# A finer rank for every step of a stage, and eight products of zeros at the start, in a Toeplitz mixer with FFN

## The chip, the cores and the metric

The kernel runs on one core of a Trainium2 chip. The time is the device time of one execution in microseconds (us). Each core has five engines that run side by side, each with its own queue that is worked off strictly in order: TensorE (PE, products into PSUM), VectorE (DVE), ScalarE (ACT), GpSimd (POOL) and SyncE (SP, which here only issues loads and stores). Weight loads of PE are shown as PEld; they overlap the products.

## The reference

The input is x with 4 batches of 2048 tokens of 256 numbers, in float32. One layer is computed:

```python
x = x + attn(_layernorm(x))
x = x + ffn(_layernorm(x))

# attn, a gated Toeplitz mixer
uv = jax.nn.silu(x @ uv_w)                 # (.., 512)
u, v = jnp.split(uv, 2, axis=-1)
out = (u * _tno(v, rpe_params)) @ o_w

# _tno: a convolution over the 2048 tokens of each channel, both directions
a = concatenate([t_zero, t_pos, 0, t_neg]) # 4096 taps per channel
y = irfft(rfft(a) * rfft(v, n=4096))[:2048]

# taps: a small network of the position, times a decay
h = pos @ rpe_pos_w
for i in range(3):
    h = silu(ln(h, w[i], b[i])) @ rpe_fc_w[i]
taps = silu(ln(h, ..)) @ rpe_out_w * 0.99 ** |pos|

# ffn: 8 groups of 1024 tokens, each with its own two matrices and no nonlinearity
h1 = einsum('gmh,goh->gmo', xg, W1) + b1
h2 = einsum('gmo,gho->gmh', h1, W2) + b2
```

## The kernel before, in words

**Tiling.** Tokens lie on the 128 partitions. A batch is cut into four quarters of 512 tokens (q = 0 to 3), the 256 channels into two halves (h = 0, 1). The long convolution is cut, by additions on DVE, into 8 "rings" (r = 0 to 7), each a transform of length 256 done as products with a constant matrix.

**Stages.** All are Python functions that only record operations:

- `rpe_network` (line 540): the position network for all 4096 positions, four layers one after the other. A layer is two products `ph`, their squares and copies on ACT, sixteen small products `pvar` that sum the squares, an inverse root on DVE (`inverse_root`, line 524, three Newton steps of small operations), its spread `ne` (DVE), eight transposes `pr` (PE), two products on DVE and the activation `z` (ACT), which feeds the next `ph`.
- `rpe_transform` (line 617): the taps' transform by rings: products `hp`, a DVE product `tr`, products `pa`, and copies into the constant tables `amd` and `am0` to `am6`.
- `stage_a` (line 495), for each batch and quarter: load x (`xa`), mean and variance (`statistics`, line 367; on DVE for batch 0, on ACT for the others), the power -1/2 on POOL (`rs`), normalisation on ACT (`xn`), eight transposes (`pt_a`), copies (`xnt`), the products `pv` with the value half of uv_w, silu, and sums on POOL (`c`).
- `prepare` (line 759), for each batch and half: 16 pieces of DVE additions that make the eight rings.
- `gate` (line 781): the products `pu` and silu, the gate `gt`.
- `stage_b` (line 791): for each ring a `forward` (products `pf` and, on DVE, the complex product with the table: two products `y` and `far`, then two sums into `y`), a `backward` (products `acc`) and an `after` on DVE; `end` combines the rings on DVE into four tiles `tk`, which POOL multiplies into the gates.
- `stage_w` (line 722), for each of the 8 FFN groups: the two matrices are multiplied with each other, `pw`, in four chunks (o = 0, 2, 4, 6) of 256 KB of W1 and 256 KB of W2 each. A chunk has `WB = 2` buffers; its W1 half is shifted by a bias on ACT before the four products. The result is `wt`.
- `stage_d` (line 927), for each batch and quarter: load x again, products `po` with o_w, add, layernorm as in stage a, transposes `pt_d`, products `pff` with `wt`, add, store.

**What sets the order.** The order of the instructions is made by a planner, `issue_order` (line 220). It knows which operation reads what another writes, the buffers of each pool, and an estimated duration of each (`Operation.cost`, line 116). It then plays the program through: of all operations whose inputs and buffers are there, the one that can start earliest goes next, and among those that can start at the same time the one of the lowest rank. A rank is a number from the table `PLACE`, plus 20 for each batch:

```python
at, _, _, k = min((at, ops[k].engine == "POOL", rank[k], k) for w in waiting.values() for k in w if (at := earliest(k)) is not None)
```

The ranks also set the order in which the tiles of a pool get their buffers. In the kernel before, all operations of one call of a stage share one rank: loading, statistics, transposes and products of a quarter of stage a, the load of the matrix, the products and the DVE steps of a ring. Only `prepare`, `end`, `stage_w` and `stage_d` are cut into pieces (at each `yield`) that have ranks of their own.

The resulting order is what the chip runs. All instructions are issued at line 1019, so the profile shows that line for nearly all of them, and tiles tell them apart.

Of the kernel before, what the change touches and what calls it, by code (L numbers as in the profile page):

```python
# [106 lines left out]
class Operation:  # L107
# [8 lines left out]
    def cost(self, method):  # L116

        n, psum = columns(self.outs[0]), [a.space == PSUM for a in self.ins]
        if self.dma:
            return (400 if self.engine == "SP" else 460), n * P * 4 / 250  # L120
# [20 lines left out]
class Pool:  # L141
# [5 lines left out]
    def tile(self, shape, dtype, name, **kw):  # L147
# [5 lines left out]

PLACE = {
    "a first": (-99.0, -98.0, -97.0, -96.0),
    "a": (1.74, -2.67, 2.51, 4.46),
    "b": (
        (6.26, 12.16, 4.1, 8.11, 8.37, 13.79, 12.58, 14.11),
        (10.46, 20.27, 15.97, 19.01, 18.94, 18.98, 20.74, 20.97),
    ),  # L160
    "d": (
        (25.35, 27.7),
        (26.25, 28.74),
        (30.44, 33.54),
        (29.38, 31.46),
    ),
    "d last": (
        (42.27, 25.3),
        (65.21, 140.66),
        (46.22, 27.3),  # L170
        (61.26, 28.3),
    ),
    "e": (
        (14.31, 18.21, 18.05, 16.77, 63.85, 71.2, 77.59, 18.72, 12.6, 21.84, 13.2),
        (20.2, 20.5, 20.8, 19.37, 21.4, 39.89, 22.0, 22.54, 22.6, 28.52, 26.75),
    ),
    "e last": (20.2, 100.83, 20.8, 21.1, 21.4, 111.26, 22.0, 22.3, 22.6, 22.9, 23.2),
    "f": (
        (2.08, 2.91, 1.13, 2.05, 4.0, 3.57, 6.5, 6.26),
        (4.04, 18.16, 13.91, 14.02, 14.8, 14.19, 17.79, 18.04),  # L180
    ),
    "g first": (
        (-95.0, 1.77, -95.0, -40.12),
        (-95.0, -95.0, -95.0, -95.0),
    ),
    "g": (
        (6.27, 12.71, 15.72, 5.68),
        (13.81, 10.75, 16.06, 24.4),
    ),
    "p first": (21.76, -4.4, -4.1, -3.8, -3.5, -23.28, -84.19, -2.6, -2.3, -2.0, -1.7, -1.4, -1.1, -0.8, -0.5, 5.66),  # L190
    "p": (
        (55.79, 1.74, 22.08, 23.91, 1.63, 19.64, 38.78, 19.76, 4.06, 16.19, 4.2, 33.43, 39.59, 10.38, 4.51, 33.61),
        (14.03, 5.6, 11.32, 67.54, 11.67, 6.8, 14.31, 16.92, 15.07, 18.9, 70.61, 20.64, 18.53, 20.4, 45.22, 86.73),
    ),
    "rpe": -100.0,
    "rpet": -10.0,
    "w": (-52.41, -95.4, 43.06, 31.0, 55.36, 77.26, 90.91, 188.4),
# [3 lines left out]
def place(stage, *i):  # L201
    if stage in ("rpe", "rpet"):
        return (PLACE[stage],)
    if stage == "w":
        return (PLACE["w"][i[0]] + 0.1 * i[1],) if i[0] < WT else (PLACE["w"][i[0]] + i[1],)
    b, *i = i
    if b == 0 and (stage in ("a", "g") or (stage == "p" and i[0] == 0)):
        stage, i = stage + " first", i[1:] if stage == "p" else i
    elif b == B - 1 and (stage == "d" or (stage == "e" and i[0] == 1)):
        stage, i = stage + " last", i[1:] if stage == "e" else i  # L210
    at = PLACE[stage]
    for n in i:
        at = at[min(n, len(at) - 1)]
    return (20 * b + at,)


# [3 lines left out]
def issue_order(ops, tags):  # L220
# [43 lines left out]
    while len(order) < len(ops):  # L264
# [5 lines left out]
        free[o.engine] = at + o.busy  # L270
        end = at + o.busy + o.tail
# [24 lines left out]
def kernel(  # L296
# [49 lines left out]
    am_c = [const.tile([P, 2, 2, 2, P], F32, name=f"am{r}") for r in range(NR)]  # L346

# [147 lines left out]
    def stage_a(b, q):  # L495
        xnt = xnts[b, q] = tok.tile([P, 2, 4 * P], F32, tag="xnt", bufs=4, name=f"xnt_{b}_{q}")
        xt = early.pop((b, q), None) or load_x(b, q, "xa")
        name = f"a{b}_{q}"
        transposed(normalized(xt, *statistics(xt, name, on_scalar=b > 0), name), xnt, name)
# [11 lines left out]
        r, j0 = divmod(2 * q, 4)  # L511
        for h in range(2):
            lo, hi = (v[:, :, i, h * P : (h + 1) * P] for i in range(2))
            c = cts[b, h]
            G.tensor_tensor(c[:, r, j0 : j0 + 2, 0, :], hi, lo, ALU.add)
            a_, b_ = (lo, hi) if r else (hi, lo)
            G.tensor_tensor(c[:, 1 - r, j0 : j0 + 2, 1, :], a_, b_, ALU.subtract)
# [22 lines left out]
    def rpe_network():  # L540
# [7 lines left out]
        early.update({(0, q): load_x(0, q, "xa") for q in range(2)})  # L548
        decay = t4("decay", "f4")[:, :NT]
        S.dma_start(decay, decays)  # L550

# [17 lines left out]
        for i in range(L + 1):  # L569
            sqs, ds = [], []  # L570
# [25 lines left out]

        z = t4("z", "i4").rearrange("p (j f) -> p j f", f=F)
# [10 lines left out]
    def load_phases():  # L608
        phs = [io.tile([P, 4, D], F32, tag="xd", name=f"ph_{i}") for i in range(2)]
# [7 lines left out]
    def rpe_transform(z, phs):  # L617
# [62 lines left out]
        for r in range(NR + 1):  # L680
            m = ring_mats(r, 0, f"rpe_{r}")
            ph = ps_f.tile([P, 2 * P], F32, tag="pf", name=f"hp{r}")
# [15 lines left out]
            for k in range(2):  # L698
# [12 lines left out]
                elif k:  # L711
                    A.copy(am_c[r - 1][:, :, :, k, :], src)
                else:
                    V.tensor_copy(am_c[r - 1][:, :, :, k, :], src)

# [6 lines left out]
    def stage_w(g):  # L722
        na, oc = INTER // P, 2
        yield
# [4 lines left out]
        S.dma_start(row, b2[g : g + 1, :].partition_broadcast(P))  # L729
        d = small.tile([P, na], F32, tag="d", bufs=2, name=f"dw_{g}")  # L730
# [4 lines left out]
        for o in range(0, na, oc):  # L735
            w1s = io.tile([P, oc, D], F32, tag="w1", bufs=WB, name=f"w1_{g}_{o}")
            S.dma_start(w1s, w1[g].rearrange("(p a) h -> p a h", a=na)[:, o : o + oc, :])
            w2s = io.tile([P, oc, D], F32, tag="w2", bufs=WB, name=f"w2_{g}_{o}")
            S.dma_start(w2s, w2t[g].rearrange("(p a) h -> p a h", a=na)[:, o : o + oc, :])
# [382 lines left out]
```

## Time and profile before

| | us |
|---|---|
| three runs | 589.31, 589.51, 590.65 (median 589.51) |
| the profiled execution | 589.18 |
| its span, first to last instruction | 587.3 |
| PE busy in the span | 563.2 (96%), 2620 records |
| DVE busy | 504.4 (86%), 1118 records |
| ACT busy | 312.8 (53%) |
| POOL busy | 149.7 (25%) |
| moved by DMA | 81.36 MB, mean 139 GB/s |

The profiled execution is one more execution, 0.3 us under the median of the three runs. A product in float32 appears as two records of PE, a transpose as one. Records overlap, so a record's own duration is longer than the time until the next one starts; where a stretch is dense, the distance of the starts is the cost. Records of one kind that follow each other are merged into one line with their number (x16).

### The profile page before, as it was taken

How to read it: one execution, taken by the hardware profiler on the slowest of the kernel's cores; microseconds unless marked ns; L12 is line 12 of the kernel's file. 1: busy time of each engine (PE TensorE's matmuls, PEld its weight loads, DVE VectorE, ACT ScalarE, POOL GpSimd, SP SyncE). 2: the span in 40 equal slices, each digit the busy share in tenths (PEclk: the TensorE clock that was granted, in tenths of full speed). 3: DMA queues.
4: the chain of work that ended last, by engine and by line, in shares of the span. 5: the costliest groups of instructions: out<-in, count | busy, mean ns of one | idle time of the engine just before them, and what ended most of it. 6: DMA issues, size and time to landing. Idle time of an engine off the chain costs nothing.

```text
span 587.3 us, 8243 instructions
## 1 busy us (share of the span) xinstructions
PE 563.2 (96%) x2620; PEld 457.3 (78%) x2620; DVE 504.4 (86%) x1118; ACT 312.8 (53%) x822; POOL 149.7 (25%) x184
## 2 busy tenths in 40 slices
PE   6899999999997999999999999999999999998797
PEld 3788565887885888787878888778888888787686
DVE  3575984999998799999986999998979999999862
ACT  2779862164322754996545728886348365112162
POOL 0154210011362211123475200106271100020420
PEclk9999999999999999999999999999999999999999
DMA  8731374555454445363541453455443543424202
GB/s 266 204 113 61 89 230 154 157 165 161 142 146 136 109 145 171 108 228 114 157 119 46 153 179 127 145 179 145 125 108 90 193 158 143 149 67 138 78 37 108
DMA packets 39987, 81.36 MB, mean 139 GB/s; under 512 B 5636, under 2 KB 7172, under 8 KB 39944
## 3 DMA queue, kind: packets, MB, share of 16 engines
q1 hardware_dynamic: 39208, 79.91, 44.2%
q10 hardware_dynamic: 736, 0.92, 0.5%
q8 instruction: 21, 0.34, 0.2%
q14 instruction: 22, 0.18, 0.1%
HBM read 72.43 MB, written 8.39 MB: 138 GB/s over the span
## 4 chain that ended last, share of the span: by engine, by line
PE 88%; DMA 7%; ACT 2%; DVE 1%; issue 1%; SPq 0%; ACTq 0%; DVEq 0%
PE acc L1019 18%; PE pf L1019 18%; PE pff L1019 9%; PE pv L1019 9%; PE po L1019 9%; PE pw L1019 7%; PE pu L1019 7%; DMA w<-in_L_ffn_W_dram 6%; PE pt_a L1019 2%; PE pa L1019 2%; PE pt_d L1019 2%; PE ph L1019 2%; PE pvar L1019 1%; PE hp L1019 1%; PE pr L1019 1%; DMA lag_t<-in_lag_rows_dram 1%
## 5 line engine op out<-in xcount | busy, mean ns | idle before, releaser
L1019 PE MATMUL acc<-mats,y 128*128 128x256 f32 (+1 forms) x512 | 114.7, 367 | 0.0
L1019 PEld LDWEIGHTS acc<-mats,y 128*128 128x128 f32 x512 | 91.7, 190 | 14.0 <-issue 2.1
L1019 PE MATMUL pw<-w,w 128*128 128x256 f32 x256 | 65.9, 388 | 11.5 <-DMA w<-in_L_ffn_W_dram 9.7
L1019 POOL TENSOR_TENSOR gt<-gt,tk 128x512 f32<-128x512 f32 x32 | 44.8, 1411 | 122.8 <-DVE tk L1019 122.8
L1019 POOL TENSOR_TENSOR c<-v 128x256 f32<-128x256 f32 x64 | 55.5, 894 | 56.2 <-ACT v L1019 45.8
L1019 PEld LDWEIGHTS pw<-w,w 128*128 128x128 f32 x256 | 46.8, 194 | 21.9 <-ACT w L1019 13.6
L1019 PE MATMUL pv<-uvw,xnt 128*128 128x256 f32 x256 | 60.7, 382 | 0.0
L1019 PE MATMUL po<-ow,gt 128*128 128x256 f32 x256 | 60.2, 379 | 0.0
L1019 ACT ACTIVATE w<-w,dw 128x256 f32<-128x256 f32 x64 | 29.6, 502 | 56.9 <-DMA w<-in_L_ffn_W_dram 56.9
L1019 PE MATMUL pu<-xnt,uvw 128*128 128x512 f32 x128 | 59.8, 592 | 0.0
L1019 PE MATMUL pf<-ra,mats 128*128 128x256 f32 x256 | 58.9, 380 | 0.0
L1019 PE MATMUL pff<-wt,xn 128*128 128x256 f32 x256 | 58.0, 380 | 0.3 <-ACT xn L1019 0.3
L1019 PEld LDWEIGHTS pv<-uvw,xnt 128*128 128x128 f32 x256 | 47.4, 190 | 8.3 <-ACT xnt L1019 1.2
L1019 PEld LDWEIGHTS pf<-ra,mats 128*128 128x128 f32 x256 | 48.2, 190 | 7.0 <-issue 0.5
L1019 PEld LDWEIGHTS pff<-wt,xn 128*128 128x128 f32 x256 | 48.1, 190 | 6.8 <-ACT xn L1019 0.6
L1019 PEld LDWEIGHTS po<-ow,gt 128*128 128x128 f32 x256 | 47.8, 190 | 7.0 <-issue 1.0
L1019 DVE TENSOR_TENSOR y<-y,far 128x256 f32<-128x256 f32 x128 | 51.8, 445 | 0.2
L1019 POOL TENSOR_TENSOR rs_a<-ve_a,mhalf 128x4 f32<-128x4 f32 x16 | 19.8, 1236 | 113.3 <-ACT ve_a L1019 105.2
L1019 POOL TENSOR_TENSOR rs_d<-ve_d,mhalf 128x4 f32<-128x4 f32 x16 | 16.6, 1037 | 115.4 <-ACT ve_d L1019 99.2
L1019 DVE TENSOR_TENSOR y<-pf,am 128x512 f32<-128x512 f32 x56 | 38.3, 684 | 6.5 <-PE pf L1019 5.0
L1019 ACT COPY e<-acc 128x512 f32<-128x512 f32 x24 | 14.0, 584 | 50.5 <-PE acc L1019 43.6
L1019 DVE TENSOR_TENSOR far<-pf,am 128x512 f32<-128x512 f32 x56 | 38.1, 681 | 0.2
(151 smaller groups left out, 1022.0 us busy)
## 6 DMA issues: line engine op xcount, KB each, us to landing
mats<-in_mats_dram SPq DMA_DIRECT2D x128, 256.0 KB, 2.7
w<-in_L_ffn_W_dram SPq DMA_DIRECT2D x64, 256.0 KB, 4.2
xa<-in_x_dram SPq DMA_DIRECT2D x18, 512.0 KB, 3.7
xd<-in_x_dram SPq DMA_DIRECT2D x14, 512.0 KB, 3.5
out_dram<-xd SPq DMA_DIRECT2D x12, 512.0 KB, 2.7
mats_rpe<-in_mats_dram SPq DMA_DIRECT2D x8, 256.0 KB, 4.1
row<-in_L_ffn_b_dram SPq DMA_DIRECT2D x8, 128.0 KB, 4.8
ph<-in_phases_dram SPq DMA_DIRECT2D x4, 256.0 KB, 5.5
```

The costliest lines, as they stand in the source:

```text
L1019: ops[k].call(*ops[k].args, **ops[k].kw)
```

## The change

Four things are edited.

1. Eight products of a tile of zeros (128x256) into a PSUM tile that nothing reads are put at the head, with rank -199. The PSUM tile shares the one buffer of `pw`. A memset of 128x256 on DVE makes the zeros.
2. `PLACE` becomes a flat table with dotted keys. `place` looks up the longest key that is in the table, with " first" for batch 0 and " last" for batch 3, and falls back to shorter keys ("b.1.4.p" to "b.1.4" to "b.1" to "b").
3. Each stage is cut finer: stage a into load (x), statistics and normalisation (n), transposes (t), products (v) and sums (c); a ring into the matrix load (m), the products (p) and the DVE steps (y), forward (f) and backward (b); stage w into loads (l), bias (d), products (m) and the final sum (s), for each chunk; stage d into load, output products (o), statistics (n), transposes (t), FFN products (f) and store (s); each network layer and each ring of the table's transform has a rank of its own.
4. The planner's estimates: a DMA takes its real number of partitions at 270 instead of 128 at 250, and a product that starts in the first 7500 ns counts double.

No operation of the computation is removed or added; buffers and their numbers stay.

```diff
-            return (400 if self.engine == "SP" else 460), n * P * 4 / 250
+            return (400 if self.engine == "SP" else 460), n * self.outs[0].shape[0] * 4 / 270
...
 PLACE = {
-    "a first": (-99.0, -98.0, -97.0, -96.0),
...
-    "rpe": -100.0,
-    "rpet": -10.0,
-    "w": (-52.41, -95.4, 43.06, 31.0, 55.36, 77.26, 90.91, 188.4),
+    "a.0 first": -99, "a.0.n first": -118, "a.0.x first": -89,
+    "a.1.c first": -67, "a.1.n first": -84, "a.1.t first": -89, "a.1.v first": -88, "a.1.x first": -83,
+    "a.2.c first": -87, "a.2.n first": -80, "a.2.t first": -86, "a.2.v first": -37, "a.2.x first": -97,
+    "a.3 first": -96, "a.3.n first": -107, "a.3.v first": -94,
...
+    "f.1.2.p": 16, "f.1.2.y": 12, "f.1.3": 14.02, "f.1.3.y": 9, "f.1.5.m": 33, "f.1.5.p": 14.5, "f.1.5.y": 14.19,
...
+    "rpe": -100,
+    "rpe.0": -135,
+    "rpe.1": -134,
...
+    "w.0": -52.31, "w.0.l.1": -52.21, "w.0.l.2": -52.11, "w.0.l.3": -52.01, "w.0.m.1": -52.21, "w.0.m.2": -70,
...
+    "warm": -199,
 }
...
-def place(stage, *i):
...
+def place(key, b=0):
+    first, last = [key + " first"] * (b == 0), [key + " last"] * (b == B - 1)
+    for k in (*first, *last, key):
+        if k in PLACE:
+            return (20 * b + PLACE[k],)
+    return place(key.rpartition(".")[0], b) if key else (20 * b,)
+
+
+
+COLD, WARM_UP = 7500, 8
...
-        free[o.engine] = at + o.busy
-        end = at + o.busy + o.tail
+        busy = o.busy * (2 if o.engine == "PE" and at < COLD else 1)
+        free[o.engine] = at + busy
+        end = at + busy + o.tail
...
         xnt = xnts[b, q] = tok.tile([P, 2, 4 * P], F32, tag="xnt", bufs=4, name=f"xnt_{b}_{q}")
+        at(f"a.{q}.x", b)
         xt = early.pop((b, q), None) or load_x(b, q, "xa")
         name = f"a{b}_{q}"
-        transposed(normalized(xt, *statistics(xt, name, on_scalar=b > 0), name), xnt, name)
+        at(f"a.{q}.n", b)
+        xns = normalized(xt, *statistics(xt, name, on_scalar=b > 0), name)
+        at(f"a.{q}.t", b)
+        transposed(xns, xnt, name)
+        at(f"a.{q}.v", b)
...
         def forward(r):
+            at(f"f.{h}.{r}.m", b)
             m = ring_mats(r, 0, f"{nm}_{r}")
+            at(f"f.{h}.{r}.p", b)
...
+            at(f"f.{h}.{r}.y", b)
             y = ys[r] = t2(f"y_{nm}_{r}", "y").rearrange("p (k r c) -> p k r c", k=2, r=2)
...
+    at("warm")
+    zeros = const.tile([P, 2 * P], F32, name="zeros")
+    V.memset(zeros, 0.0)
+    warm = ps_w.tile([P, 2, D], F32, tag="w", name="warm")
+    for _ in range(WARM_UP):
+        T.matmul(warm[:, 0, :], zeros[:, :P], zeros, start=True, stop=True)
```

## The prediction

> **What bounds the kernel now.** I read four views in this order: the page's first two parts, the chain of waits, TensorE's (PE's) own waits, and the timelines of the places where PE loses time.
>
> ```profile
> PE 563.2 (96%) x2620; PEld 457.3 (78%) x2620; DVE 504.4 (86%) x1118; ACT 312.8 (53%) x822; POOL 149.7 (25%) x184
> PE   6899999999997999999999999999999999998797
> PE 88%; DMA 7%; ACT 2%; DVE 1%; issue 1%; SPq 0%; ACTq 0%; DVEq 0%
> ```
> PE is the bound: the chain that ended last is 88% PE. In dense stretches a record of 256 columns starts every 0.216 us (a product is two such records; a transpose is one record of 0.108). Laid end to end at that rate the 2620 records take 550.5 us, so 36.8 of the 587.3 us are lost, and that is all that a new order can win.
>
> ```profile
> PE pw L1019 <- DMA w<-in_L_ffn_W_dram: 9.7, 7, 2.1
> PE ph L1019 <- DMA lag_t<-in_lag_rows_dram: 5.3, 1, 5.3
> PE pr L1019 <- DVE ne L1019: 2.3, 1, 2.3
> ```
> These are waits alone. The rest is rate, and the timeline of the first 26 us shows it:
>
> ```profile
> 5.27 3.75 PE L1019 MATMUL ph<-lag_t,w 4*128 4x512 f32 x4 [5.27 <-DMA lag_t<-in_lag_rows_dram]
> 8.94 3.58 PE L1019 MATMUL pvar<-par,sq 128*128 128x4 f32 x16
> 12.85 2.04 PE L1019 MATMUL pw<-w,w 128*128 128x256 f32 x4 [0.33 <-DMA w<-in_L_ffn_W_dram]
> 17.19 1.94 PE L1019 MATMUL pr<-ident,ne 128*128 128x128 f32 x8 [2.30 <-DVE ne L1019]
> 20.63 1.41 PE L1019 MATMUL pw<-w,w 128*128 128x256 f32 x4
> 21.88 1.88 PE L1019 MATMUL ph<-z,bd 128*128 128x512 f32 x4
> 24.02 1.84 PE L1019 MATMUL pvar<-par,sq 128*128 128x4 f32 x16
> ```
> The same sixteen variance products take 3.58 us at 8.94 and 1.84 at 24.02: until 21.2 us PE runs at half rate, though the row of the granted clock shows full speed throughout. When the second network layer starts at 21.88, PE has done products worth 6.9 us: 15.0 us are lost. Later losses: 1.5 us at 74, 1.0 at 145, 4.6 at 183 to 191, 0.9 at 307, 5.6 at 537 to 548, 0.9 near the end and 4.2 after the last product's start. From 192 to 536 PE is dense; nothing can be won there, only lost.
>
> ```profile
> 184.43 1.97 PE L1019 MATMUL pw<-w,w 128*128 128x256 f32 x8 [1.53 <-DMA w<-in_L_ffn_W_dram]
> 187.72 1.97 PE L1019 MATMUL pw<-w,w 128*128 128x256 f32 x8 [1.32 <-DMA w<-in_L_ffn_W_dram]
> 190.97 1.53 PE L1019 MATMUL pw<-w,w 128*128 128x256 f32 x6 [1.29 <-DMA w<-in_L_ffn_W_dram]
> ```
> A chunk of FFN weights has two buffers. From the end of one chunk's products to the start of those two chunks later it takes about 5.0 us (182.7 to 187.72), through release, two loads and ScalarE's (ACT's) scaling. Where fewer than 5.0 us of products lie between, PE waits for the rest.
>
> **The change, part by part.** No work is removed; one memset (0.27 us, as the row of the 128x256 memset) and eight products of zeros are added. In the new instruction order I lay PE's products end to end at the rates above.
>
> *Front, -3.6 us.* The zeros run from about 1.3 us, when PE waits anyhow. All cold they take 16 x 0.43 = 6.8 us and end at 8.1; if the rate doubles after 4 us of them, at 6.5. So the first ph starts 1.2 to 2.9 later than 5.27. What ends last before the second layer's ph is ACT. Its queue now holds two weight scalings ahead of the first squares, and both normalisations and copies of quarters 0 and 3 ahead of the table load and z. On SP decay, biases and two weight loads go ahead of x: same bytes, other places, so x of quarter 0 lands 3 to 4 us later than 7.1, quarter 3 at 11.5 to 12.5. Three of quarter 3's statistics stand before the first Newton step on VectorE (DVE), which thus starts at 13.0 to 14.1 instead of 12.56; that covers the later ph. GpSimd's power for quarter 3 now stands behind two steps of group 0's bias, loaded by about 14.5: 0.4 and 1.0 us more, so 16, within Newton's 3.8 us. Quarter 3's scale is there at 16.5; then 2.08 of normalisation, a copy of 0.56, 1.28 of
>
> ```profile
> 18.91 1.28 ACT L1019 ACT_TABLE_LOAD   x1
> 20.20 1.52 ACT L1019 ACTIVATE z<-d,par 128x512 f32<-128x512 f32 x2
> ```
> and 0.76 of z: the second ph at 21.25. By then the new order has issued 9.9 us of products, so 11.4 are lost instead of 15.0. Bounds: -5.4, if z is ready at 19.5 (the loads landing early); -0.6, if PE is cold again until about 26 us (half of 4.7) and quarter 3 lands 0.6 later. I take the middle, with PE warm: the gaps that I count between 8 and 17 us are at most 2 us each, and those of the old kernel after 21.2 (up to 2.1 us) cost no rate.
>
> [...]
>
> *First weight group, +1.4.* Group 0's third chunk is now loaded first, and chunks 0, 1 and 3 share one buffer, 4.3 us of products after each other: three waits of 0.7 by the 5.0 us, 1.5 each by the 5.8 that the old kernel needed at 75.75, against 1.5 us lost today. Ends +0.6 and +3.0.
>
> *145 us, -1.0.* A transpose waits for a copy; in the new order eight products stand ahead of it. Ends -1.0 and 0.
>
> *Group 2, -1.3.* Chunks 0 and 1 are now loaded 13.8 us ahead, 2 and 3 follow 1.7 us after: 5.0 - 1.7 = 3.3 us lost instead of 4.6. Ends -1.8 (the gate products aren't ready earlier) and 0.
>
> *307 us, -0.7.* Group 4's third chunk follows 6.5 us of products after its buffer's last use, not 4.3. Ends -0.9 and 0.
>
> *End, 0.* Chunk distances differ, but the waits again sum to 5.7, and the DVE chain beneath them is as long:
>
> ```profile
> 545.36 4.64 DVE L1019 TENSOR_TENSOR tk<-p 128x512 f32<-128x512 f32 x4
> 552.20 0.69 DVE L1019 TENSOR_TENSOR xd<-xd,po 128x512 f32<-128x512 f32 x1 [2.21 <-PE po L1019]
> ```
> From the end of ring 1's last accumulation (530.8) DVE needs 19.2 us to the last tk, PE has 13.4 us of products; the 5.7 between stay. Ends -2.0 (some output products move up) and +1.5 (one tk now stands before that chain).
>
> *Dense stretch, +1.0.* Between a ring's forward product and its backward product lie two multiplies and two sums on DVE. Its rows:
>
> ```profile
> 102.68 0.68 DVE L1019 TENSOR_TENSOR far<-pf,am 128x512 f32<-128x512 f32 x1
> 103.39 0.76 DVE L1019 TENSOR_TENSOR y<-y,far 128x256 f32<-128x256 f32 x2
> 104.93 0.69 DVE L1019 TENSOR_TENSOR y<-pf,am 128x512 f32<-128x512 f32 x1 [0.77 <-PE pf L1019]
> ```
> Started 0.27 us after the product (104.66 to 104.93), 0.60 + 0.60 + 0.75 and a hop of some 0.15 make 2.4 us. The old order leaves at least 3.3 us of products between. The new one leaves 2.6 at four places (ring 2 of batch 1's second half; ring 3 of batch 3's first; rings 1 and 4 of its second). With DVE 86% busy an operation in progress (0.6) can push each past its slot. Ends 0 and +3.0 (0.75 each); 0.25 each is nearest to the rows.
>
> All other moves of ranks leave products, DMAs and their number as they are and stand within those slots; I cost them at nothing. Their cover is PE's dense queue.
>
> Sum: -3.6 + 1.4 - 1.0 - 1.3 - 0.7 + 0 + 1.0 = -4.2, on the profiled execution's 589.18 (span 587.3 and 1.9 around it): 585.0. That execution lies 0.3 under the median of the three runs: 585.3 forecast.
>
> **The rivals.** *Much more is won.* If the second ph comes at 19.5, group 0's loads keep pace (+0.6 instead of +1.4) and no slot is missed: -4.2 - 1.8 - 0.8 - 1.0 = -7.8, and with the end's -2.0 -9.8: 579.7 to 581.7. For it: PE's row shows no later obstacle. Against: three in-order queues must all be early.
>
> *The zeros do nothing.* PE is cold again at 17 us; front -0.6 to -1.2, total -1.2 to -1.8: 587.7 to 588.3. For it: 9.4 us of ph, variance and pw products from 5.27 on did not raise the rate. Against: those fill 4 rows or 4 columns, the zeros 128 by 256.
>
> *Nothing is won.* DVE is nearly as full as PE; if it can't follow, the front's gain returns as a wait for tk before each batch's output products: 589.5. Against: DVE idles 5.3 us at 189 and 9 us between 89 and 101, both on PE, and moves up with it.
>
> *Slower: a y too late for its slot.* Mechanism: in the 2.6 us slots DVE's in-order queue holds a full other step (a prepare or a tk) ahead of the y, and PE stands for y's whole 2.1 us, with all its queue. Four slots cost 8.4 instead of 1.0: 592.7. It decides from the third such slot on (-5.2 + 6.3). For it: DVE's dense rows. Against: in the old kernel slots of 3.5 us never made PE wait.
>
> **How the numbers follow.** Chances: forecast 0.50 (own range 582 to 587.7), more won 0.18, zeros without effect 0.12 (half of it under 587.7), nothing won 0.06, slower 0.14. 0.3% of 589.5 is 1.8 us, about what a measurement of this kernel can tell from no change. Faster: 0.50 + 0.18 + 0.06 = 0.74; same 0.12; slower 0.14. All terms at their best give 579, at their worst 596; leaving out 0.06 below and 0.12 above, the range is 579.5 to 591.
>
> **What would show it.** Front right: variance products of layer 0 at full rate (about 1.8 us for sixteen), the second ph near 21 with quarter 0's pv done before it. Wrong: transposes and pv at half rate at 17 us, or the second ph after 22.5. Group 0: three waits of PE for weights between 60 and 80 us. Group 2: one wait of about 3.3. Slots: PE waits for DVE's y, none of which exists now. The prediction is wrong if such waits pass 4 us together, or if the front gains under 2 or over 5.5.

## The result and the profile after

The change makes the kernel slower. Four runs of it took 597.96 to 600.89 us (median 598.99), four runs of the kernel before on the same chip 588.31 to 590.65 (median 589.41): ratio 1.0171, 95% interval 1.0149 to 1.0193, some 10 us. The profiled execution took 598.10, its span is 596.3 us, 9.0 more than before. The forecast was 585.3, the range 579.5 to 591.0.

The page of the changed kernel, its lines of busy time, of the granted clock by slices and of the chain:

```profile
PE 573.1 (96%) x2636; PEld 463.9 (78%) x2636; DVE 503.1 (84%) x1119; ACT 314.2 (53%) x822; POOL 146.9 (25%) x184
PEclk8899999999999899999999999999999999999899
PE 85%; DMA 7%; ACT 4%; DVE 2%; issue 1%; SPq 1%; ACTq 0%; DVEq 0%
```

The row of the granted clock in the kernel before:

```profile
PEclk9999999999999999999999999999999999999999
```

PE's busy time grew by 9.9 us although only eight products came in (6.1 us), and the row of the granted clock has 8s where it had only 9s: part of the added "work" is the same work at half rate. PE's waits, where there were mainly weights before (9.7 us):

```profile
PE pw L1104 <- DMA w<-in_L_ffn_W_dram: 5.3, 3, 3.1
PE pw L1104 <- ACT w L1104: 4.6, 2, 2.5
PE pvar L1104 <- ACT sq L1104: 1.9, 1, 1.9
PE hp L1104 <- DMA mats_rpe<-in_mats_dram: 1.4, 1, 1.4
PE acc L1104 <- DMA mats<-in_mats_dram: 1.0, 1, 1.0
```

The weights' 9.9 us (5.3 and 4.6) come in longer pieces, and three short waits are new. No wait of PE for a `y` is there.

To see where the 9.0 us are, I work out what PE loses in each stage: from each record's start to the next one's, less 0.216 us for 256 columns (in proportion for others, with 0.108 for products of four columns too), which is what dense stretches take; the head before the first record, the tail after the last, and all products of zeros count as lost.

| stage, us from the start | before | after | difference | forecast |
|---|---|---|---|---|
| 0 to 60: network, stage a of batch 0 | 15.6 | 17.3 | +1.7 | -3.6 |
| 60 to 100: group 0, table's transform | 1.4 | 5.3 | +3.9 | +1.4 |
| 100 to 180 | 1.6 | 1.1 | -0.5 | -1.0 |
| 180 to 205: group 2 | 4.9 | 5.1 | +0.3 | -1.3 |
| 205 to 520: dense, 307 us | 2.4 | 3.0 | +0.7 | +0.3 |
| 520 to the end | 11.3 | 14.3 | +3.0 | 0 |
| sum | 37.0 | 46.0 | +9.0 | -4.2 |

The same measure is used for the runs below. The front's timeline on PE:

```profile
1.18 6.08 PE L1104 MATMUL warm<-zeros 128*128 128x256 f32 x16 [1.18 <-DVE zeros L1104]
7.20 1.98 PE L1104 MATMUL ph<-lag_t,w 4*128 4x512 f32 x4
11.11 1.87 PE L1104 MATMUL pvar<-par,sq 128*128 128x4 f32 x8 [1.93 <-ACT sq L1104]
...
13.83 1.71 PE L1104 MATMUL pvar<-par,sq 128*128 128x4 f32 x8
15.39 3.76 PE L1104 MATMUL pw<-w,w 128*128 128x256 f32 x8
18.95 1.39 PE L1104 MATMUL pt_a<-ident,xn_a 128*128 128x128 f32 x8
...
25.14 1.98 PE L1104 MATMUL ph<-z,bd 128*128 128x512 f32 x4 [0.84 <-ACT z L1104]
```

The zeros did raise the rate: the four `ph` records take 1.98 us instead of 3.75. But eight variance products then take 1.87 us, which is half rate again (sixteen took 1.84 at 24 us before), and so do eight `pw` records (3.76 instead of 1.9). The second network layer starts at 25.14; it started at 21.88 before, and 21.25 was forecast.

And the granted clock, in stretches of 3.4 us that begin or end near its changes (it is at 0.50 from 9.42 to 19.66 us and for 3.41 us each from 193.74, 548.73 and 555.55; columns: busy time and records of PE, PEld, DVE, ACT and POOL, granted clock, share of the DMA engines, GB/s):

```profile
2.60:6.00 3.40, 3.40 (x9) 2.66 (x8) 1.80 (x8) 0.00 (x0) 0.00 (x0) 1.00 1.01 311
6.00:9.40 3.40, 3.18 (x10) 1.42 (x8) 0.00 (x0) 1.03 (x1) 0.61 (x3) 1.00 0.75 148
9.40:12.80 3.40, 1.69 (x8) 1.70 (x9) 1.05 (x4) 3.09 (x7) 0.00 (x0) 0.50 1.02 403
12.80:16.20 3.40, 3.40 (x13) 3.13 (x14) 2.55 (x16) 0.84 (x2) 1.44 (x3) 0.50 1.08 236
16.20:19.60 3.40, 3.40 (x11) 2.67 (x11) 3.20 (x16) 1.75 (x4) 1.21 (x2) 0.50 1.04 272
...
190.30:193.70 3.40, 0.78 (x4) 0.73 (x5) 3.30 (x4) 0.91 (x2) 2.02 (x2) 1.00 0.79 239
193.70:197.10 3.40, 3.40 (x10) 2.69 (x9) 1.85 (x2) 0.91 (x2) 3.40 (x4) 0.51 0.08 24
545.30:548.70 3.40, 1.30 (x7) 0.86 (x6) 3.40 (x8) 0.91 (x2) 0.00 (x0) 1.00 0.76 237
548.70:552.10 3.40, 3.40 (x10) 2.66 (x9) 3.40 (x7) 0.91 (x2) 0.00 (x0) 0.50 0.08 25
552.10:555.50 3.40, 1.24 (x6) 0.75 (x4) 3.30 (x5) 0.67 (x2) 2.37 (x2) 0.99 0.73 193
555.50:558.90 3.40, 3.02 (x7) 2.52 (x8) 1.43 (x1) 1.15 (x3) 3.40 (x3) 0.51 0.47 117
```

The 1.00 of the first row can't be taken as it stands: its nine records of zeros in 3.4 us run at half rate, as PE did until 21.2 us in the kernel before, where the row shows full speed too. The granted clock falls to 0.50 at 9.4 us for 10.2 us, and three more times for 3.4 us each; in the 3.4 us ahead of these three PE was busy for 0.78, 1.30 and 1.24 us. The kernel before waits about as long at the end (1.80, 1.05 and 2.12 us, with eight records of 1.97 us between), but there PE is busy for 1.93 to 1.97 us of each of three such stretches, and the clock stays at 1.00:

```profile
540.20:543.60 3.40, 1.97 (x8) 1.44 (x8) 3.40 (x9) 1.04 (x3) 0.00 (x0) 1.00 0.56 174
543.60:547.00 3.40, 1.97 (x8) 1.44 (x8) 3.29 (x6) 0.77 (x2) 0.81 (x1) 1.00 0.54 137
547.00:550.40 3.40, 1.93 (x9) 1.75 (x10) 2.99 (x2) 1.10 (x3) 3.40 (x3) 1.00 0.55 177
```

### The profile page after: what moved, and what is told of

The parts are those of the page before. It is cut to its first block, busy times and chain, and to the rows that moved or that the text cites. A ratio compares the mean times of both kernels' runs of the same rounds, so it can differ in the third digit from the quotient of the medians.

```text
span 596.3 us, 8254 instructions
## 1 busy us (share of the span) xinstructions
PE 573.1 (96%) x2636; PEld 463.9 (78%) x2636; DVE 503.1 (84%) x1119; ACT 314.2 (53%) x822; POOL 146.9 (25%) x184
## 4 chain that ended last, share of the span: by engine, by line
PE 85%; DMA 7%; ACT 4%; DVE 2%; issue 1%; SPq 1%; ACTq 0%; DVEq 0%
PE pf L1104 17%; PE acc L1104 16%; PE pff L1104 9%; PE po L1104 9%; PE pw L1104 8%; PE pu L1104 8%; PE pv L1104 8%; DMA w<-in_L_ffn_W_dram 5%; PE pt_a L1104 2%; PE pt_d L1104 2%; PE pvar L1104 1%; PE pa L1104 1%; ACT w L1104 1%; PE ph L1104 1%; DMA mats_rpe<-in_mats_dram 1%; DMA mats<-in_mats_dram 1%
## 5 line engine op out<-in xcount | busy, mean ns | idle before, releaser
L1104 PE MATMUL acc<-mats,y 128*128 128x256 f32 (+1 forms) x512 | 116.9, 367 | 1.6 <-DMA mats<-in_mats_dram 1.0
L1104 PE MATMUL pw<-w,w 128*128 128x256 f32 x256 | 69.6, 415 | 10.8 <-DMA w<-in_L_ffn_W_dram 5.3
L1104 PEld LDWEIGHTS pw<-w,w 128*128 128x128 f32 x256 | 51.8, 209 | 24.2 <-ACT w L1104 13.9
L1104 POOL TENSOR_TENSOR c<-v 128x256 f32<-128x256 f32 x64 | 50.0, 808 | 70.8 <-ACT v L1104 64.4
L1104 PE MATMUL pu<-xnt,uvw 128*128 128x512 f32 x128 | 61.0, 594 | 0.0
L1104 PE MATMUL pf<-ra,mats 128*128 128x256 f32 x256 | 60.4, 379 | 0.0
L1104 POOL TENSOR_TENSOR rs_d<-ve_d,mhalf 128x4 f32<-128x4 f32 x16 | 18.2, 1136 | 113.6 <-ACT ve_d L1104 97.7
L1104 ACT ACTIVATE xn_d<-xd,nb_d,rs_d 128x256 f32<-128x256 f32 x56 | 29.3, 589 | 16.2 <-DVE nb_d L1104 11.5
```

The costliest lines, as they stand in the source:

```text
L1104: ops[k].call(*ops[k].args, **ops[k].kw)
```

## The experiments

The ratio of each run is taken to the kernel before, measured on the same chip in the same session; its median was 589.3 to 592.5 us from session to session.

**Without the zeros.** The planner still counts them, so the order is that of the changed kernel (`warms` holds the numbers of the eight products).

```diff
         for k in issue_order(ops, tags):
+            if k in warms:
+                continue
             ops[k].call(*ops[k].args, **ops[k].kw)
```

> The changed kernel in its own instruction order, without the eight products of zeros (the memset stays, and the output is the reference's). Theory 'ScalarE sets the front': in the changed kernel ScalarE's first square starts at 10.48 us, behind a table load and two weight scalings that waited for weights until 8.37; without the zeros the first layer's products start near 5.3 instead of 7.2, at half rate, and end near 9, still before 10.48. So the time stays: 597.5 to 600. Rival 'the zeros are what makes the front late': the zeros end 1.9 us after the first operands have landed, and the whole front moves up by that: 596 to 597.3. Rival 'the zeros keep the rate up': without them more of the first 20 us runs at half rate: 600.5 to 602.

Measured: 599.63 us, ratio 1.0138 (1.0095 to 1.0181). The interval holds the changed kernel's 1.0171 and the prices of the first two theories, so the time alone does not part these. In the trace the first layer's products start 1.6 us earlier (5.61 instead of 7.20) and the second layer 0.5 earlier, at 24.66 instead of 25.14. In the changed kernel's order the zeros are worth nothing, or cost a little: most of what they delay waits for ScalarE anyhow.

**The zeros alone, in the kernel before.**

```diff
+        nc.vector.memset(zeros, 0.0)
+        for _ in range(8):
+            nc.tensor.matmul(warm[:, 0, :], zeros[:, :P], zeros, start=True, stop=True)
         for k in issue_order(ops, tags):
```

> The kernel before in its own order, with eight products of 128x256 zeros put ahead of everything on TensorE (the planner does not know of them). Theory 'the rate is taken back': the zeros raise the rate at about 6 us, the first layer's products run at full rate from 7 to 9, and the four-row products and the four-column variance products that follow let the granted clock fall to 0.5 again, as in the changed kernel at 9.5 us; second layer within 0.7 us of 21.9; total 589 to 591. Rival (my forecast's assumption) 'it stays warm': sixteen variance products in about 1.8 us and the second layer at 18.5 to 20.5: 586.5 to 588.2. Rival 'the zeros only delay': everything in the front 1.9 us later: 591 to 592.

Measured: 589.65 against 591.76, ratio 0.9964 (0.9941 to 0.9986): 2.1 us faster, by the ratio inside the range of "it stays warm", but the trace shows the other theory's picture. The rate was raised for the first layer, the clock fell to 0.50 at 10.4 for 10.2 us, the second layer starts at 21.49. In that profile the first 60 us gain 0.4. It shows one of the slowest executions of this kernel, though (591.58; its ten took 587.43 to 591.89); I take the rest of the 2.1 to come from executions in which the rate is up sooner (the zeros take 6.58 us in this profile and 5.14 in that of the run with zeros and three buffers below); that was not shown.

**Zeros in three waits for weights.**

```diff
+    FILL, fill = {(2, 4): 6, (7, 0): 4, (7, 4): 5}, {}
...
+            if (g, o) in FILL:
+                fill[len(ops)] = pw[:, 0, :], FILL[g, o], o == 0
...
         for k in issue_order(ops, tags):
+            if k in fill:
+                tile, n, start = fill[k]
+                for _ in range(n):
+                    nc.tensor.matmul(tile, zeros[:, :P], zeros, start=start, stop=start)
```

> The changed kernel with products of zeros added in three waits of TensorE for FFN weights: six ahead of the third chunk of group 2 (the wait of 3.1 us at 190), four ahead of group 7's first chunk (2.1 us at 546), five ahead of its third (2.5 us at 553), 0.43 us each, added to the same sums, in which they change nothing. Theory 'clock': the waits stay, but the half rate that followed each of them for 3.4 us (granted clock 0.50 from 193.6, 548.6 and 555.6) is gone, 1.7 us each: 593 to 595.5 against 599.0, and the granted clock stays 1.00 from 20 us to the end. Rival 'the end is bound by VectorE': only the 1.7 at 193.6 are won, and TensorE waits longer for tk at the end: 596.5 to 598. Rival 'the clock falls for another reason' (it falls with no regard to what TensorE does): no change or slower, 598.5 to 601.

Measured: ratio 1.0061 (1.0036 to 1.0087), 6.5 us less than the changed kernel's 10.1; against the run without zeros, on the same chip, 3.3 us less (596.31 and 599.63). The stretches around the same waits:

```profile
190.30:193.70 3.40, 3.19 (x15) 2.47 (x13) 3.30 (x6) 0.59 (x2) 0.92 (x1) 1.00 0.76 200
193.70:197.10 3.40, 2.69 (x11) 2.12 (x12) 2.95 (x2) 1.23 (x3) 3.40 (x3) 1.00 0.38 108
...
550.80:554.20 3.40, 3.40 (x17) 3.00 (x16) 3.30 (x7) 0.00 (x0) 0.62 (x1) 1.00 0.51 113
554.20:557.60 3.40, 1.93 (x9) 1.42 (x8) 3.18 (x2) 1.81 (x4) 3.40 (x3) 1.00 0.64 196
```

The clock is 1.00 from 20 to 565 us, where in the changed kernel it was 0.50 three times for 3.4 us. Only products in PE's idle time were added, so in these three places it was the idleness that took the rate away, and fifteen products that compute nothing make the kernel faster. The price of the half rate is nearer to 3.6 us than to the 5.1 that I worked out: against the run without zeros PE loses 1.2 less around 190 (4.1 and 5.3) and 2.5 less at the end (12.8 and 15.2), since some of the slow products were followed by another wait for the next chunk, which grows when they are fast.

**Group 0's ranks as before.**

```diff
+for g in [0]:
+    step = 0.1 if g < 3 else 1
+    for k in range(4):
+        PLACE[f"w.{g}.l.{k}"] = PLACE[f"w.{g}.m.{k}"] = PLACE[f"w.{g}"] + step * k
+    PLACE[f"w.{g}.l"] = PLACE[f"w.{g}.d"] = PLACE[f"w.{g}"]
+    PLACE[f"w.{g}.s"] = PLACE[f"w.{g}"] + step * 4
```

> The changed kernel with the ranks of FFN group 0 alone as they were before (one step of 0.1 for each chunk, loads, scalings and products of a chunk at one rank). Theory 'ranks of group 0': the four waits of TensorE between 66 and 96 us (1.0, 1.1, 0.9 for its chunks, 1.5 for a matrix of the table's transform queued behind them on SP) shrink from 5.1 in all to 1.5 to 2.5: 596 to 597.5. Rival 'group 1': those waits come from group 1's products, which now stand 6 to 10 us of work later and hold both buffers; then the waits stay within 1 us of 5.1: 598.2 to 600.

Measured: 597.25 us, but on a chip where the kernel before took 591.76: ratio 1.0082 (1.0059 to 1.0105), 5.3 us less than the changed kernel's 10.1, more than expected; 2.4 us under the run without zeros on that chip. Between 60 and 100 us PE loses 1.2 instead of 5.3, with one wait for weights left, so those waits were group 0's. Another comes later, for group 3's chunk; with a new wait for a `p` (1.4) the stage from 100 to 180 loses 3.4 instead of 1.1:

```profile
69.98 1.97 PE L1112 MATMUL pw<-w,w 128*128 128x256 f32 x8 [0.91 <-DMA w<-in_L_ffn_W_dram]
110.58 1.10 PE L1112 MATMUL pw<-w,w 128*128 128x256 f32 x4 [1.21 <-DMA w<-in_L_ffn_W_dram]
```

**The squares ahead of the weight scalings.**

```diff
+        order = issue_order(ops, tags)
+        late = [k for k in order if k in scaled]
+        order = [k for k in order if k not in scaled]
+        i = order.index(last_copy[0]) + 1
+        order[i:i] = late
```

(`scaled`: the two scalings of group 1's first chunk and its first product; `last_copy`: the copy of the first layer's second half.)

> The changed kernel with three instructions moved in the front and nothing else: ScalarE's two scalings of the first weight chunk go behind the first layer's squares and copies, and the one product that needs them behind the second half's variance products. Then ScalarE's first instruction waits for nothing but the first layer, so its table load can run early, as before the change (there at 1.75 us), and the first square comes near 8.2 instead of 10.48. Theory 'a chain of several': the statistics of x (loaded by 11.75) still stand before the first Newton step on VectorE, and TensorE's half rate stays, so the second layer's first product comes only 0.3 to 1.2 us earlier than 25.1: 8.4 to 9.6 us over the kernel before, against 10 (ratio 1.0171) of the changed kernel. Rival 'ScalarE's queue is the front's loss': all 2.3 us come through: 7.2 to 7.8 over the kernel before.

Measured: ratio 1.0119 (1.0092 to 1.0146), 7.0 us over the kernel before, and the interval (5.4 to 8.6) reaches into both theories' numbers. The trace goes with "a chain of several": the second layer starts at 24.56, 0.6 earlier than 25.14, and the first 60 us lose 0.7 less. That the time moved further than the trace explains stays unexplained. What it shows plainly is ScalarE's start, in the changed kernel first:

```profile
8.37 1.28 ACT L1104 ACT_TABLE_LOAD   x1 [8.37 <-DMA w<-in_L_ffn_W_dram]
9.67 0.91 ACT L1104 ACTIVATE w<-w,dw 128x256 f32<-128x256 f32 x2
10.48 0.57 ACT L1104 ACTIVATE sq<-ph 128x512 f32<-128x512 f32 x1
```

and in this run:

```profile
1.75 1.28 ACT L1116 ACT_TABLE_LOAD   x1 [1.75 <-issue]
8.21 0.60 ACT L1116 ACTIVATE sq<-ph 128x512 f32<-128x512 f32 x1 [5.17 <-PE ph L1116]
```

With the scalings at the head of the queue, the table load too stands behind the weights' landing.

**More zeros in the front.** Five ahead of the variance products, one between their halves, four ahead of the first transposes:

```diff
+                if i == 0 and c % 4 == 0:
+                    fill[len(ops)] = (None, 1, False) if c else (warm, 5, True)
                 T.matmul(pv[:, c, :]
...
+        if b == q == 0:
+            fill[len(ops)] = (None, 4, False)
         transposed(xns, xnt, name)
```

> The changed kernel with ten more products of zeros in the first 18 us, where TensorE stands: five between the first layer's products and the variance products, one between the halves of these, four ahead of the first transposes; they change no sum. Theory 'rate': the granted clock does not fall to 0.5 at 9.5 us, or comes back 3.4 us or more earlier than 19.7; the transposes and with them ScalarE's copy, the second normalisation and z come earlier, second layer at 23 to 24 instead of 25.1: 7.4 to 8.6 us over the kernel before, against 10. Rival 'loads and queues': the second layer stays within 0.5 us of 25.1: 9.4 to 10.6 over. Rival 'the zeros are in the way': they delay variance products and transposes by more than the rate gives back: 10.8 to 12 over.

Measured: ratio 1.0159 (1.0128 to 1.0189), 9.4 us over; by time none of the three is excluded. By the trace the theory "rate" holds: the clock is 1.00 in the front from 5.9 us on, where it was 0.50 for 10.2 us, eight `pw` records take 1.97 us instead of 3.76, and the second layer starts at 23.66:

```profile
9.40:12.80 3.40, 2.65 (x16) 2.14 (x15) 1.56 (x7) 3.39 (x7) 0.00 (x0) 1.00 1.03 408
12.80:16.20 3.40, 3.40 (x21) 3.09 (x21) 3.09 (x21) 2.11 (x5) 1.77 (x4) 1.00 1.08 245
16.20:19.60 3.40, 3.16 (x19) 2.64 (x18) 2.22 (x8) 1.82 (x5) 0.87 (x2) 1.00 1.03 307
```

The front loses 1.5 less than in the changed kernel's profile. The stages behind it lose 2.3 more, as in the other changed kernel on this chip (the squares first: 3.4 more), and the kernel before was 2.8 slower here too. That points to the chip rather than to the edit, but no run separates the two. At full rate the second layer is still 1.8 later than before the change: the rate is not all of the front.

**The front's ranks as before,** with the zeros, the planner's estimates and all other ranks as changed:

```diff
+for k in list(PLACE):
+    if k.startswith(("a.", "g.")) and k.endswith(" first") or k.startswith(("rpe", "w.0", "w.1")):
+        del PLACE[k]
+PLACE |= {"a.0 first": -99, "a.1 first": -98, "a.2 first": -97, "a.3 first": -96, "rpe": -100, "rpet": -10}
...
```

> The changed kernel with the ranks of the front alone as before: stage a, gates and first additions of batch 0, the position network, the table's transform and FFN groups 0 and 1; the eight zeros, the planner's estimates and every rank of the dense part and of the end stay as changed. Theory 'front and group 0': second layer at 19 to 22 us, one wait of about 1.5 us instead of four between 60 and 100; of the 10 us 5 to 7 go: ratio 1.005 to 1.0085, with the half rate after the waits at about 190 and 550 still there. Rival 'the dense part and the end are the loss': under 3 us go, 1.012 or more.

Measured: ratio 1.0030 (1.0001 to 1.0058). Some 8.3 us of the 10.1 are gone, more than I expected. The first 60 us lose 12.7 instead of 17.3, less than the 15.6 of the kernel before, and 60 to 100 lose 1.5. The half rate is still there, for 3.4 us behind the wait at 183 to 187 and for 6.8 us near 550. In the front the first x is normalised at 10.85 (15.87 in the changed kernel), and PE has transposes and `pv` where it had weight products:

```profile
9.42 3.04 PE L1119 MATMUL pvar<-par,sq 128*128 128x4 f32 x16
12.31 1.95 PE L1119 MATMUL pt_a<-ident,xn_a 128*128 128x128 f32 x8
14.08 3.35 PE L1119 MATMUL pv<-uvw,xnt 128*128 128x256 f32 x8
17.27 1.04 PE L1119 MATMUL pr<-ident,ne 128*128 128x128 f32 x8
18.15 1.89 PE L1119 MATMUL pv<-uvw,xnt 128*128 128x256 f32 x8
19.88 1.88 PE L1119 MATMUL ph<-z,bd 128*128 128x512 f32 x4
```

**That and the zeros in the three waits:** the edits of the two runs together.

> The changed kernel with the front's ranks as before (the run g4_old_front, 1.003 of the kernel before) and the products of zeros in the three waits ahead of group 2's third chunk and group 7's first and third (the run e3_fill, which brought the changed kernel from 1.0171 to 1.0061). Theory 'two independent losses': the half rate after the three waits (granted clock 0.50 for 3.4 us after the wait at 183 to 187 and for 6.8 us near 550 in g4_old_front) goes here too, 5 us: ratio 0.993 to 0.997, a little faster than the kernel before, since the zeros at the head are kept. Rival 'the same time twice': with the front mended the end is bound by VectorE and the fill wins 1.7 us at most: 1.000 to 1.003.

Measured: 588.02 against 589.28, ratio 0.9986 (0.9964 to 1.0007), between the two theories. The clock is 1.00 from 20 to 565 us, and PE loses 1.8 less around 185 and 3.3 less at the end than in the run with the old front alone; by the ratios it is 2.6 less, give or take 2.

**All places mended at once** in the changed kernel's own order: group 0's ranks, the three fills, the squares first, and on SP the two first loads of x ahead of decay, biases and weights.

```diff
+        order = [k for k in order if k not in moved]
+        i = order.index(decay_op[0])
+        order[i:i] = moved
```

> The changed kernel with every place mended at once that the trace names: group 0's ranks as before, products of zeros in the three waits ahead of group 2's third chunk and group 7's first and third, ScalarE's squares ahead of the first weight scalings, and the two first loads of x ahead of decay, biases and weights on SP, as x stood before the change. Theory 'the loss is the sum of these places': ranks of group 0 -4, half rate after three waits -5, front -1 to -2.5 of the 10 us that the changed kernel lies over the kernel before: 3 under to 0.5 over it, ratio 0.995 to 1.001. Rival 'they come back': the time saved at one place is waited for at the next loads (the ring matrix at 420, the chunks of groups 3 and 7), and 3 to 6 us over the kernel before stay: 1.005 to 1.010.

Measured: 592.77 against 592.48, ratio 1.0005 (0.9987 to 1.0024): the loss is the sum of the named places, within what the expectation allowed. In the front little was won, though (second layer at 24.45). The second chunk's scaling still stands ahead of the normalisations and now waits until 14.39 for its weights, and quarter 0's copy again waits 2.1 us for its transposes:

```profile
14.39 0.51 ACT L1140 ACTIVATE w<-w,dw 128x256 f32<-128x256 f32 x1 [2.10 <-DMA w<-in_L_ffn_W_dram]
15.07 2.08 ACT L1140 ACTIVATE xn_a<-xa,nb_a,rs_a 128x256 f32<-128x256 f32 x4 [0.17 <-DVE nb_a L1140]
19.24 0.58 ACT L1140 COPY xnt<-pt_a 128x512 f32<-128x512 f32 x1 [2.10 <-PE pt_a L1140]
```

**Three buffers for the chunks of weights,** in the kernel before (`WB = 3`), then with the zeros, then with three zeros more behind the first variance products.

> The kernel before with three buffers instead of two for the chunks of FFN weights (WB = 3; the planner spreads the chunks accordingly). Theory 'release to product': TensorE's waits for weights at 74 (1.5 us), 183 to 191 (4.6) and 307 (0.9) come from two buffers and some 5.0 to 5.6 us from a chunk's release to the products of the chunk that follows in it; with three buffers at least 4 of these 7.0 us go, while the 5.6 near the end stay (there VectorE's chain to the last tk is longer than TensorE's work): 4 to 6.5 us under the kernel before, ratio 0.989 to 0.993. Rival 'SP's queue': a chunk loaded earlier stands ahead of ring matrices and of x in SP's order and the waits move there: 0.996 to 1.004.

> Three buffers for the chunks and the eight zeros at the head, both in the kernel before. Theory 'they add': the zeros alone gave 2.1 us (0.9964, interval 0.9941 to 0.9986), three buffers 4 to 6.5: ratio 0.985 to 0.990. Rival 'the zeros' gain is the same time': the first microseconds saved are waited for again at the first weights, so no more than three buffers alone, within 0.002 of that run.

> The kernel before with the eight zeros at the head, three buffers for the chunks of FFN weights, and three more products of zeros behind the first layer's variance products, where TensorE waited 2.7 us for the first weights. Theory: the rate is up sooner in more of the executions, whatever the place of the 3.4 us steps of the clock; 0.5 to 2 us under the same kernel without the three (0.9951): ratio 0.992 to 0.994. Rival 'they stand in the way' where the weights are not late and the rate is half: 0.996 to 0.999.

Measured: 0.9983 (0.9970 to 0.9996), 0.9951 (0.9935 to 0.9967) and 0.9953 (0.9930 to 0.9977). The third buffer does what it should at 74 and 307 us and around 185 (0.5 instead of 1.4 lost between 60 and 100, 2.7 instead of 4.9 around 185). But the front loses 2.5 more, 2.3 of them between 20 and 60 us, where the planner now puts weight products among the network's (one wait of 1.2 for `ne` at 43), and the stage from 520 us on loses 2.8 more. There the waits for chunks before 555 us shrink by 2.8, but 5.4 come in behind 570, where the last transposes stand for ScalarE:

```profile
PE pt_d L1019 <- ACT xn_d L1019: 4.0, 1, 4.0
```

The mean granted clock of this profile is 0.997 (1.000 in the kernel before), which would be 3.5 us at 0.50 in a span of 589.3; I put some 1.7 of the 5.4 down to that. The third of these runs has the same wait of 4.0 us and shows the half rate behind it: from 575.12 on eight transposes take 2.16 us (eight take 1.04 at 17.27 in the run with the old front) and sixteen `pff` records 4.32 instead of the 3.62 at 559.90. So 1.0 us is left of my 4 to 6.5; the rival's price was right and its mechanism (SP's queue) was not. The zeros add their 1.9; in the profile of the second run they take 5.14 us (6.58 in that of the zeros alone), the variance products behind run at full rate and the second layer starts at 18.86:

```profile
8.16 1.95 PE L1025 MATMUL pvar<-par,sq 128*128 128x4 f32 x16
...
18.86 1.88 PE L1025 MATMUL ph<-z,bd 128*128 128x512 f32 x4
```

The three more zeros change nothing that can be measured. With 588.94 against 592.21 the second of the three, and with it the third, beats both kernels.

## Why the prediction was wrong

**Front, -3.6 forecast, +1.7 measured.** Its own sign of being wrong came, the second ph after 22.5 (25.14). The step that failed is "I take the middle, with PE warm". I had counted single gaps and found none over 2 us. The longest is 1.93 us (9.18 to 11.11), and the clock fell 0.24 us into it: from 6.0 to 9.4 PE had a record running for 3.18 of 3.40 us, 1.2 of them zeros and nearly all the rest four-row `ph` products, and from 9.42 the clock was 0.50. With five more products of zeros from 8.44 on, in the run with more zeros, it stayed at 1.00. Nor did PE's next full stretch bring it back: from 12.8 to 16.2 PE was busy all the time, half of it with variance products (four columns), and the clock was 0.50 until 19.66. Restored rate is worth 1.5 us of the 3.9 between 21.25 and 25.14 (23.66 in the run with more zeros). The second step that failed is ScalarE's: I named the scalings ahead of the squares and gave them no price (0.6 us by the run with the squares first). The third is the sum "16.5; then 2.08 of normalisation": quarter 3's normalisation stands behind a copy of quarter 0, which waited 2.0 us for transposes that stand behind the weight products. I had listed that copy and let it wait for nothing. That these and x's later landing make up the remaining 1.8 is read from the trace and not shown one by one; that the front's ranks as a whole cost 4.6 us there is shown by the run with the old ones (17.3 and 12.7). Up to the second ph PE lost 15.2 us where 11.4 were forecast; another 1.4 more than before is lost between there and 60 us, where nothing was forecast, 1.0 of it in two waits for `ne` (0.66 at 34 and 0.38 at 56 us).

**First weight group, +1.4 forecast, +3.9 measured.** The three waits came where they were forecast (70, 77 and 84 us; 1.02, 1.10 and 0.88, with 5.4 to 5.6 us from a buffer's last product to the next, for which I had 5.0 to 5.8). From start to start they lose 3.5 us, 0.6 more than the 2.9 behind the +1.4. What I missed is the matrix of the table's transform at 94, 1.45 us: its load is queued on SP behind loads of the same chunks, which wait for their buffers until 87. The queue's other waiting loads had to be followed too.

**Group 2 and the end.** Here the waits are right: 3.3 from start to start at 189 for 3.3 forecast, and 5.5 in three pieces at the end for 5.7. The failed step is to take the same sum of waits for the same loss. In one piece of 3.13 us at 190, and in pieces of 2.10 and 2.54 at the end, they left PE busy for 0.78, 1.30 and 1.24 of 3.4 us, and the products behind ran at half rate for 3.4 us each time: +0.3 for -1.3 and +3.0 for 0. Counting single gaps, as I did, cost the forecast some 4 to 5 of the 13.2 us by which it missed the span (1.5 in the front, 2.6 to 3.6 after the three waits).

**145 us, 307 us, dense stretch.** The waits at 145 and 307 went as forecast (0.2 left at 307), though 100 to 180 gained 0.5 of 1.0 only. The slots of `y` held: no wait of PE for one. The wait that the dense stretch did get, 0.96 us at 421, is for a ring matrix on SP, which no step had looked at.

**The chance of slower** was 0.14, with y's slots as its mechanism; it came by another way. The rival "the zeros do nothing" had the front's picture (half rate at 17 us) with too small a price, as it left the longer queue on ScalarE out. No run shows the -1.2 at the far end of its front, which was an estimate of mine; the front lost 1.7 more instead, and the transposes started every 0.21 us until 19.59 and every 0.11 from 19.74 on. The 4 us of zeros after which the rate would double were assumed: in the changed kernel's profile the zeros' records start every 0.43 us until 6.03 and every 0.21 from there, 4.85 us after the first. Two of the prediction's smaller figures are off without bearing on the outcome: by its own terms warm zeros would end at 6.7 us, not 6.5 (7.2 measured), and VectorE idles 7.1 us, not 9, between 89 and 101 in the kernel before.

By ratios the whole adds up like this: the zeros alone -2.1, the finer ranks of the front +8.3 (from 1.0030 to 1.0171), all else between 0.9964 and 1.0030 +3.9, of which the half rate after three waits is 2.6 to 3.6. The planner's changed estimates are in that last part; no run sets them back alone. The remainder is within the error of these runs (about 2 us each), so whether the finer ranks of the dense part win or lose anything stays open.

## What to carry to other kernels

Price what runs behind PE's waits, not the waits alone: here waits of 3.13, 2.10 and 2.54 us were each followed by 3.4 us at a granted clock of 0.50, up to 1.7 us more each (half of 3.4; 2.6 to 3.6 for the three by the runs that filled them). Single gaps don't tell: a wait of 2.12 us at the end of the kernel before left its clock at 1.00. A wait that can't be removed is better filled with products of zeros, as the runs here show, or split, as group 2's waits in the kernel before suggest (1.53, 1.32 and 1.29 us, clock 1.00 throughout), than merged (3.13 us). When a finer order moves an instruction to the head of an in-order queue, look up when its operand lands, and price everything that then stands behind it, table loads (at 8.37 us here instead of 1.75) and copies of other stages too. Where a product is bound by a chain on other engines, as at this kernel's end, more buffers can just move the wait.

## What the runs showed of the hardware that I had not expected

- **Waits that left the clock up, and waits that did not.** In the changed kernel 3.4 us with PE busy for 0.78, 1.24 and 1.30 us were followed by a clock of 0.50; in the kernel before, 3.4 us with 1.93 to 1.97 us by 1.00. The run without zeros has both at the end, 1.65 us with the clock at 1.00 behind it and 0.93 us with 0.51 behind it:

```profile
545.20:548.60 3.40, 1.65 (x8) 1.12 (x6) 3.40 (x8) 0.30 (x1) 0.00 (x0) 1.00 0.65 195
548.60:552.00 3.40, 2.94 (x13) 2.40 (x14) 3.40 (x8) 1.52 (x4) 0.00 (x0) 1.00 0.40 114
552.00:555.40 3.40, 0.93 (x5) 0.48 (x3) 3.29 (x5) 0.25 (x1) 1.28 (x1) 1.00 0.76 169
555.40:558.80 3.40, 2.55 (x6) 2.13 (x7) 2.52 (x2) 1.56 (x4) 3.40 (x3) 0.51 0.43 144
```

- **The way back up.** In the changed kernel's front, 3.4 us at 0.50 with PE busy for 1.69 us were followed by another 0.50, and so were 3.40 us half filled with variance products; 3.40 us of weight products and transposes (16.2 to 19.6) were followed by 1.00. Behind the three waits it took 3.41 us with PE busy for 3.02 to 3.40.
- **The rate changes at another time in each run.** In nine of the profiles with zeros at the head these start at 1.18 or 1.19 us, but their sixteen records take anything from 5.14 to 6.58 us. The kernel before varies with its clock too: 29 runs of it in one session spread over 589.5 to 597.0 us, the nine with a granted clock of 1.000 at 591.2 in the mean and the five with 0.996 or less at 594.4. That is part of the spread; the nine alone still reach from 589.5 to 593.5. The kernel with all places mended, whose waits are filled, stayed within 592.2 to 593.8 in 12.
- **Which products went with a higher rate.** Products of zeros raised it (at 6.03 us in the changed kernel), and in three waits they kept it. Products of four rows or four columns did not: in the kernel before they ran without a pause from 5.27 to 12.5 us, and the four `pw` records at 12.85 still took 2.04 us. Transposes did: in the run with zeros and three buffers PE ran nothing but transposes from 14.78 to 17.99 us, the first eight in 1.94 us, and the four `pw` records behind them took 1.03.
